# A fused four-layer kernel on one core: its first loads made anew, and two first-layer products in a row

## The chip, the cores and the metric

The kernel runs on one core of a Trainium2 chip. The metric is the device time of one execution in microseconds. The core has five engines with a queue each: TensorE (PE in the profile; its weight loads are a row of their own, PEld), VectorE (DVE), ScalarE (ACT), GpSimd (POOL) and SyncE (SP, which here only issues transfers). Transfers (DMAs) are issued from the queues of SP, ACT and POOL.

## The reference, cut to what matters

There are 64 sequences of 64 tokens, 512 wide, in float32. Four layers follow each other, each with a residual:

```python
x = x + einsum('bsi,bio->bso', x, W[id]) + b[id][:, None, :]          # layer 0: one of 16 weight matrices per sequence
x = x + x @ W1.T + ((x @ A[ad].T) @ Bm[ad].T) * scal[ad]               # layer 1: shared weight, rank-16 adapter per sequence
q, k, v = x @ Wq.T, x @ Wk.T, x @ Wv.T                                 # layer 2: attention
q, k = rope(rms(q), kv_len + t), rope(rms(k), kv_len + t)
# k, v are written into paged caches; each token attends to the last 256 positions
x = x + softmax(q @ k_all.T * SCALE + window_mask) @ v_all @ Wo.T
x = x + x @ w3[subj] + b3[subj]                                        # layer 3: one of 8 64x64 matrices per sequence
```

Four integers per sequence steer this: the layer 0 matrix, the adapter, the layer 3 matrix, and the length of its cache. A table of 257 page numbers per sequence says where its cache lies.

## The kernel before, in words

**Tiles.** The 4096 tokens are 32 tiles of 128 tokens, two sequences each. A first half (to some 545 us) does layers 0 and 1 and the projections of layer 2; a second half does attention and layer 3. The change touches only the start of the first half.

**The order is written out by hand.** Nothing is reordered: each engine runs its instructions in the order in which the program text meets them. An instruction that waits holds up all that stands behind it in its engine's queue.

**Groups.** The tiles go in groups of 1, 1, 2, 4, 4, ... (`GROUPS`): tile 0, tile 1, tiles 2 and 3, tiles 4 to 7, and so on. Groups smaller than the next one are called short here. The main loop (L709 ff. before) takes group g through layer 1 and, spread between, the next group through layer 0. For a tile `i0` of the next group and a tile `i` of this one:

- `layer0(i0)`, L244 to 255: 8 matmuls into a PSUM bank (each is two matmul instructions, so x16 in the trace), L249; ACT copies the bank to `s0`, L252; POOL adds the bias to x into `x1`, L260 (`add_bias`).
- `turn0(i0)`, L267 to 274: PE transposes `s0` (L273), DVE adds it to `x1` (L274). Only now is layer 0 of the tile done.
- `turn_x2(i)` (L654) transposes the layer 1 output; `product` (L140) multiplies it by `wq` for an earlier tile (`pq`) and by `wkv` (`pk`); `keep_kv(i)` and `parts_q` norm and rotate k and q (L120 to L135: ACT, DVE and POOL in turns).
- `layer1(tiles)`: the adapter's first product `pxa` (L620) needs `x1` of every tile of the group; DVE masks it into `xa` (L625); `p1 = x1 @ w1` (L635); the adapter's second product adds `bo @ xa` (L643); ACT copies the bank out (L648).

Where a group is short, some tiles of the next one have no `i`; there `turn0(i0)` follows `layer0(i0)` at once, and PE's transposes wait for ACT's copy of `s0`.

**Side work on DVE.** `rotation(0)` (L366 to 397) makes the sine and cosine for tiles 0 to 7, 20 DVE instructions and two on ACT; `scalars()` (L399 to 407) prepares the norm's gains. `windows()` (L427 ff.) is a generator that computes from the page tables which cache rows to fetch; `other(i)` (L697) takes two of its steps per tile: in the trace its set-up and 5 "picks" (L470) stand with tile 1, 10 picks with tile 2, 11 with tile 3.

**Loads and their order.** SP's queue issues the integers (`tok1`, L198), x of tile 0 (L222), then weights: for tile 0 in four chunks per sequence (`load_w0(0, KC, (nc.sync, nc.scalar))`), the first sequence's from SP, the second's from ACT. Then `w1`, adapter rows (`ao`, L293), x and weights of tile 1, `wkv`, and so on. ACT's queue first issues four small loads: `idcol` (the 64 matrix numbers, one per partition, L200), `toki` (all 256 integers, to all 128 partitions, L202), `invf` (L204) and `gain` (L205); after the weights come `kvi` and `tabi` (L322 and L323). POOL gathers the bias rows `brow` (L212, needs `idcol`) and the adapter rows `bo` (L301, needs `toki`).

Transfers of SP and ACT share eight completion semaphores in turn, in the order of the program text. The ninth transfer reuses the first one's, so its issue waits until that one has landed.

Of the kernel before, what the change touches and what calls it, by code (L numbers as in the profile page):

```python
# [22 lines left out]
KC = D // 128  # L23
# [36 lines left out]
def body(ctx: ExitStack, tc: tile.TileContext, a: dict, out: bass.AP):  # L60
# [124 lines left out]
    with ExitStack() as pa:  # L185
# [13 lines left out]
        idcol = su.tile([B, 1], I32, name="idcol")  # L199
        nc.scalar.dma_start(idcol, a["toks"][:, 0:B].rearrange("o b -> b o"))  # L200
        toki = su.tile([128, 4, B], I32, name="toki")
        nc.scalar.dma_start(toki.rearrange("p k b -> p (k b)"), a["toks"].partition_broadcast(128))  # L202
        invf = su.tile([128, HALF], F32, name="invf")
        nc.scalar.dma_start(invf, a["invf"].partition_broadcast(128))  # L204
        nc.scalar.dma_start(  # L205
            gain.rearrange("p k h f -> p (k h f)"), a["gains"].partition_broadcast(128)
        )
        make_identity(nc, ident)
        pidx = su.tile([128, 1], I32, name="pidx")
        P.iota(pidx, pattern=[[0, 1]], base=0, channel_multiplier=1)  # L210
        brow = su.tile([B, D], F32, name="brow", tag="valp")
# [12 lines left out]
        def load_w0(i, parts=1, queues=(nc.sync, nc.sync)):  # L224

            w0s[i] = []
            for b, queue in zip((2 * i, 2 * i + 1), queues):
                w = wp.tile([128, KC, D], F32, name="w")
                r = queue.value_load(tok1[0:1, 0, b : b + 1], min_val=0, max_val=E - 1)
                for n in range(parts):  # L230
                    cs = slice(n * KC // parts, (n + 1) * KC // parts)
                    queue.dma_start(
                        w[:, cs], a["W0"][bass.ds(r, 1)].rearrange("a (c p) o -> p (a c) o", p=128)[:, cs]
                    )
                w0s[i].append(w)
# [7 lines left out]
        def layer0(i, bias=True):  # L243

            p0 = bank("p0")
            for c in range(KC):
                for h in range(2):
                    hs = slice(h * T, (h + 1) * T)
                    TE.matmul(p0[hs, :], xs[i][:, c, hs], w0s[i][h][:, c, :], start=c == 0, stop=c == KC - 1)  # L249
            w0s.pop(i)  # L250
            s0 = s0s[i] = wk.tile([128, D], F32, name="s0")
# [15 lines left out]
        def turn0(i):  # L267
# [4 lines left out]
            for c in range(KC):  # L272
                TE.transpose(pt[:, c * 128 : (c + 1) * 128], s0[:, c * 128 : (c + 1) * 128], ident)  # L273
            V.tensor_tensor(x1, pt.rearrange("p (c t) -> p c t", c=KC), x1, ALU.add)  # L274
# [43 lines left out]
        kvi = su.tile([128, 1], I32, name="kvi")  # L318
        tabi = su.tile([128, NBLK], I32, name="tabi")
        for h in range(2):  # L320
            hs = slice(h * B, (h + 1) * B)
            nc.scalar.dma_start(kvi[hs], a["toks"][:, 3 * B :].rearrange("o b -> b o"))  # L322
            nc.scalar.dma_start(tabi[hs], a["tab"])  # L323
# [26 lines left out]
        V.tensor_copy(adf.rearrange("p o q -> p (o q)"), toki[:, 1, :])  # L350
        V.tensor_tensor(adf, adf, bc(mine[:, None, :], [128, 8, 8]), ALU.mult)
# [47 lines left out]
        def scalars():  # L399
# [210 lines left out]
        bg, old, turns, asked, made = windows(), copies(kvd[:OLD], op, 3), {}, [], []  # L610

# [54 lines left out]
        scalars()  # L666

        biasT = su.tile([128, KC, B], F32, name="biasT")
        layer0(0, False)
        pb = bank("pb")  # L670
        for c in range(KC):
            TE.transpose(pb[:, c * B : (c + 1) * B], brow[:, c * 128 : (c + 1) * 128], ident[:B, :B])
        S.copy(biasT.rearrange("p c b -> p (c b)"), pb[:, : KC * B])
        add_bias(0)
        turn0(0)
# [21 lines left out]
        def other(i):  # L697

            next(bg, None)
# [378 lines left out]
```

## Time and profile before

| what | us |
|---|---|
| median of 9 runs | 951.18 (950.16 to 953.06) |
| the profiled execution | 950.0 |
| its span, first to last instruction | 948.0 |
| PE busy | 921.0 |
| DVE busy | 613.1 |
| ACT busy | 415.2 |
| POOL busy | 404.8 |

A span is the time from the first instruction to the last; 2.0 us of the profiled execution lie around it. In the rows of the timeline a line has the start in us, the length, the engine, the line of the kernel, the operation, what it writes and reads (buffer numbers left out), the shapes, how many instructions were merged, and in brackets how long the engine was idle before and what ended that. `p` is the bank of layer 0 (L249) or of layer 1 (L635, L643); `w` is any weight tile. PEclk is the granted share of TensorE's clock.

### The profile page before, as it was taken

The numbers are of one execution on the slowest core, as the hardware profiler recorded it, in microseconds if no ns is written. First come the engines' busy times: TensorE is split into PE (matmuls) and PEld (weight loads), VectorE is DVE, ScalarE is ACT, GpSimd is POOL, SyncE is SP. The second block draws the span as 40 slices with busy tenths as digits, with TensorE's granted clock in tenths as the row PEclk, the third lists the DMA queues.
The fourth block names the chain that finished last, engine by engine and source line by source line (L and its number), as shares of the span: only waits on it lengthen the run. The fifth ranks groups of instructions, "written<-read, shape, count | busy, mean of one in ns | idle before, by whom it ended". The sixth has DMA issues, their size and how long they took to land.

```text
span 948.0 us, 17784 instructions
## 1 busy us (share of the span) xinstructions
PE 921.0 (97%) x5397; PEld 506.6 (53%) x5397; DVE 613.1 (65%) x1736; ACT 415.2 (44%) x1084; POOL 404.8 (43%) x599
## 2 busy tenths in 40 slices
PE   5999998999999999999999999999999999999998
PEld 2343443444444444444344466766666777776665
DVE  3765898888575254441324888777777777777773
ACT  0312143122243221441213386666666666666663
POOL 3343466465544353444434464444444444444400
PEclk9999999999999999999999999999999999999999
DMA  7988999999999999999982696576666666666621
GB/s 241 363 298 304 363 403 290 389 401 317 380 385 355 384 337 380 395 350 371 403 297 111 193 326 216 174 231 201 214 199 199 199 204 204 204 207 209 209 60 46
DMA packets 133344, 260.97 MB, mean 275 GB/s; under 512 B 32737, under 2 KB 41570, under 8 KB 133250
## 3 DMA queue, kind: packets, MB, share of 16 engines
q1 hardware_dynamic: 108562, 178.61, 52.5%
q0 software_dynamic: 23280, 79.84, 25.6%
q10 hardware_dynamic: 1408, 1.39, 0.5%
q8 instruction: 43, 0.70, 0.3%
q14 instruction: 51, 0.42, 0.1%
HBM read 190.29 MB, written 69.50 MB: 274 GB/s over the span
## 4 chain that ended last, share of the span: by engine, by line
PE 72%; DVE 2%; DMA 1%; ACT 0%; issue 0%; POOL 0%; ACTq 0%
PE py L917 12%; PE po L889 8%; PE ps L842 8%; PE p L635 7%; PE pq L140 7%; PE pk L140 7%; PE ppt L875 6%; PE p L249 6%; PE pkt L823 2%; PE ppt L879 1%; PE pkt L829 1%; PE pz L929 1%; DMA w<-in_W 1%; PE pqt L174 1%; PE px L654 1%; PE pt L273 1%
## 5 line engine op out<-in xcount | busy, mean ns | idle before, releaser
L769 POOL DMA_INDIRECT kv<-kvd,idxn x128 | 126.6, 989 | 189.6 <-PE po L889 128.4
L854 ACT ACTIVATE pr<-pr,mx 128x320 f32<-128x320 f32 x256 | 140.1, 549 | 21.0 <-DVE mx L850 21.0
L249 PE MATMUL p<-w,xt 128*64 128x512 f32 x512 | 122.6, 605 | 9.3 <-DMA w<-in_W 9.3
L850 DVE CUSTOM_DVE_ANT_0 pr<-ps,mb 128x320 f32<-128x320 f32 x256 | 107.8, 487 | 25.7 <-PE ps L842 25.6
L917 PE MATMUL py<-wo,oT 128*128 128x512 f32 (+1 forms) x264 | 118.3, 591 | 1.7 <-DVE qn L128 1.7
L140 PE MATMUL pk<-wkv,x 128*128 128x512 f32 x256 | 115.4, 595 | 2.1 <-ACT x L656 2.1
L155 POOL DMA_INDIRECT st<-in_kvc,cidx x68 | 69.8, 1027 | 106.8 <-DMA kvd<-st 97.7
L635 PE MATMUL p<-w,x 128*128 128x512 f32 x256 | 113.2, 599 | 0.0
L140 PE MATMUL pq<-wq,x 128*128 128x512 f32 x248 | 111.3, 593 | 0.0
L274 DVE TENSOR_TENSOR x<-pt,x 128x512 f32<-128x512 f32 x32 | 22.0, 688 | 101.6 <-PE pt L273 91.6
L866 DVE TENSOR_SCALAR pr<-pr,sm 128x320 f32<-128x320 f32 x256 | 85.3, 395 | 2.2
L889 PE MATMUL po<-pT,kv 128*64 128x128 f32 (+1 forms) x1536 | 82.1, 278 | 0.0
L917 PEld LDWEIGHTS py<-wo,oT 128*128 128x128 f32 x264 | 47.5, 189 | 61.5 <-issue 58.4
L842 PE MATMUL ps<-kT,qT 64*128 64x320 f32 x512 | 79.2, 443 | 1.2 <-issue 1.2
L635 PEld LDWEIGHTS p<-w,x 128*128 128x128 f32 x256 | 48.2, 191 | 58.7 <-issue 56.8
L889 PEld LDWEIGHTS po<-pT,kv 128*64 128x64 f32 (+1 forms) x1536 | 68.9, 135 | 19.8 <-DVE mx L850 13.6
L249 PEld LDWEIGHTS p<-w,xt 128*64 128x64 f32 x512 | 35.5, 137 | 80.0 <-issue 72.7
L135 POOL TENSOR_TENSOR qr<-qn,sq 128x512 f32<-128x512 f32 x25 | 31.7, 1268 | 106.8 <-DVE qn L134 106.8
L140 PEld LDWEIGHTS pk<-wkv,x 128*128 128x128 f32 x256 | 46.3, 190 | 50.4 <-issue 47.3
L140 PEld LDWEIGHTS pq<-wq,x 128*128 128x128 f32 x248 | 44.9, 190 | 46.2 <-issue 46.2
L123 ACT ACTIVATE ss<-ss,epst 128x4 f32<-128x4 f32 (+1 forms) x64 | 19.1, 299 | 110.5 <-DVE ss L122 110.4
L133 DVE TENSOR_TENSOR sq<-qn,sg 128x256 f32<-128x256 f32 (+1 forms) x128 | 40.1, 355 | 40.2 <-POOL sg L110 37.5
(191 smaller groups left out, 1352.9 us busy)
## 6 DMA issues: line engine op xcount, KB each, us to landing
w<-in_W SPq DMA_DIRECT2D x62, 1024.0 KB
kvd<-st SPq DMA_DIRECT2D x68, 512.0 KB
xt<-in_xT SPq DMA_DIRECT2D x32, 256.0 KB
x2d<-x2n SPq DMA_DIRECT2D x32, 256.0 KB
kvd<-kvn SPq DMA_DIRECT2D x32, 256.0 KB
qTd<-qTs SPq DMA_DIRECT2D x32, 256.0 KB
qT<-qTd SPq DMA_DIRECT2D x32, 256.0 KB
x2r<-x2d SPq DMA_DIRECT2D x32, 256.0 KB
```

The lines of the kernel that those rows point to most:

```text
L140: TE.matmul(ps, x2s[i][:, c, :], w[:, c, :], start=c == 0, stop=c == KC - 1)
L155: P.indirect_dma_start(out=st, out_offset=None, in_=a["kvc"].rearrange("(n r) d -> n (r d)", r=2), in_offset=bass.IndirectOffsetOnAxis(ap= ...
L249: TE.matmul(p0[hs, :], xs[i][:, c, hs], w0s[i][h][:, c, :], start=c == 0, stop=c == KC - 1)
L635: TE.matmul(p1[i], x1s[i][:, c, :], w1[:, c, :], start=c == 0, stop=False)
L769: P.indirect_dma_start(out=kv[:, n, :], out_offset=None, in_=kvd, in_offset=bass.IndirectOffsetOnAxis(ap=at, axis=0),)
L842: TE.matmul(ps[g2][:, :NPOS], qT[rows, gp, b2].rearrange("p h t -> p (h t)"), kT[rows, gp, b2 * NPOS : (b2 + 1) * NPOS], start=True, stop= ...
L850: V.tensor_tensor_reduce(out=p, in0=ps[g2][:, :NPOS], in1=mb[:, b2, :], scale=-1.0, scalar=3.0e38, op0=ALU.add, op1=ALU.min, accum_out=mx[ ...
L854: S.activation(p, p, AF.Exp, bias=mx[:, g, b2 : b2 + 1], scale=-1.0, accum_out=sm[:, g, b2 : b2 + 1],)
L866: V.tensor_scalar(p, p, sm[:, g, b2 : b2 + 1], None, ALU.mult)
L875: TE.transpose(pt[:, n * 128 : (n + 1) * 128], pr[:, g, at : at + 128], ident)
L889: TE.matmul(po[b2][g2 * 64 : (g2 + 1) * 64, gp * 128 : (gp + 1) * 128], kv[rows, n, (G + g) * HD : (G + g + 1) * HD], pT[rows, c, m * 128 ...
L917: TE.matmul(py[:, fs], oT[:, c].rearrange("p b t -> p (b t)"), wo[:, c, fs], start=c == 0, stop=c == KC - 1,)
```

## The change

All line numbers here are of the kernel before.

- **The integers are spread by TensorE.** `idcol`, `toki` and `kvi` are loaded no more. DVE copies `tok1` to float32, four matmuls against a row of ones spread it over the partitions of a PSUM bank (`ptok`), and DVE copies two columns out or reads the bank itself.
- **Small loads last.** `invf`, `gain` and `tabi` move from ACT's queue to SP's, behind `wkv`. ACT's queue issues only its four chunks of the first weights.
- **First weights by chunk in turns.** `load_w0` with parts issues chunk 0 of both sequences, then chunk 1, and so on. On each queue the order stays as it was; the order in which the eight semaphores are given out changes.
- **Bias rows turned earlier.** The transposes of `brow` go ahead of the last chunk's matmuls of tile 0 (`turn_bias`); `turn0(0, 2)` transposes and adds in two halves.
- **Side work moved.** `scalars()` but for three operations, and `rotation(0)`, go from between `layer1([0])` and `layer0(1)` to behind `turn0(1)`. `windows()` takes no step with tile 1 and four with tile 2.
- **Two layer 0 runs in a row.** Where there is no `i`, the tile's `turn0` is held back until the next tile's `layer0` and `turn_x2` are out: for tiles 2, 4 and 6. `s0` gets two buffers.

```diff
         nc.sync.dma_start(tok1.rearrange("p k b -> p (k b)"), a["toks"])
-        idcol = su.tile([B, 1], I32, name="idcol")
-        nc.scalar.dma_start(idcol, a["toks"][:, 0:B].rearrange("o b -> b o"))
-        toki = su.tile([128, 4, B], I32, name="toki")
-        nc.scalar.dma_start(toki.rearrange("p k b -> p (k b)"), a["toks"].partition_broadcast(128))
-        invf = su.tile([128, HALF], F32, name="invf")
-        nc.scalar.dma_start(invf, a["invf"].partition_broadcast(128))
-        nc.scalar.dma_start(
-            gain.rearrange("p k h f -> p (k h f)"), a["gains"].partition_broadcast(128)
-        )
         make_identity(nc, ident)
...
+        one = su.tile([1, 128], F32, name="one")
+        V.memset(one, 1.0)
+        tokf = su.tile([1, 4, B], F32, name="tokf")
+        V.tensor_copy(tokf, tok1)
+        ptok = bank("ptok")
+        TE.matmul(ptok[:B, 4 * B : 4 * B + 1], tokf[:, 0, :], one[:, :1], start=True, stop=True)
+        for h in range(2):
+            TE.matmul(
+                ptok[h * B : (h + 1) * B, 4 * B + 1 : 4 * B + 2], tokf[:, 3, :], one[:, :1], start=True, stop=True
+            )
+        TE.matmul(ptok[:, : 4 * B], one, tokf.rearrange("p k b -> p (k b)"), start=True, stop=True)
+        toki = ptok[:, : 4 * B].rearrange("p (k b) -> p k b", k=4)
+        idcol = su.tile([B, 1], I32, name="idcol")
+        V.tensor_copy(idcol, ptok[:B, 4 * B : 4 * B + 1])
+        kvi = su.tile([128, 1], I32, name="kvi")
+        V.tensor_copy(kvi, ptok[:, 4 * B + 1 : 4 * B + 2])
...
+            first = [row(h) for h in range(2)] if parts > 1 else []
+            for n in range(parts):
+                cs = slice(n * KC // parts, (n + 1) * KC // parts)
+                for h in range(2):
+                    r = first[h] if first else row(h)
+                    queues[h].dma_start(
+                        w0s[i][h][:, cs],
+                        a["W0"][bass.ds(r, 1)].rearrange("a (c p) o -> p (a c) o", p=128)[:, cs],
                     )
...
             for c in range(KC):
+                if c == KC - 1 and not bias:
+                    turn_bias()
                 for h in range(2):
...
-        def turn0(i):
+        def turn0(i, parts=1):
...
+            for n in range(parts):
+                lo, hi = n * KC // parts, (n + 1) * KC // parts
+                for c in range(lo, hi):
+                    TE.transpose(pt[:, c * 128 : (c + 1) * 128], s0[:, c * 128 : (c + 1) * 128], ident)
+                V.tensor_tensor(
+                    x1[:, lo:hi], pt[:, lo * 128 : hi * 128].rearrange("p (c t) -> p c t", t=128), x1[:, lo:hi], ALU.add
+                )
...
         load_weight(wkv, "wkvT")
-        kvi = su.tile([128, 1], I32, name="kvi")
+        invf = su.tile([128, HALF], F32, name="invf")
+        nc.sync.dma_start(invf, a["invf"].partition_broadcast(128))
+        nc.sync.dma_start(gain.rearrange("p k h f -> p (k h f)"), a["gains"].partition_broadcast(128))
         tabi = su.tile([128, NBLK], I32, name="tabi")
         for h in range(2):
-            hs = slice(h * B, (h + 1) * B)
-            nc.scalar.dma_start(kvi[hs], a["toks"][:, 3 * B :].rearrange("o b -> b o"))
-            nc.scalar.dma_start(tabi[hs], a["tab"])
+            nc.sync.dma_start(tabi[h * B : (h + 1) * B], a["tab"])
...
-            V.memset(epst, EPS)
-            V.tensor_tensor(eye2, ident[:, :64], ident[:, 64:], ALU.add)
-            scale_b(0)
-
+
+        V.memset(epst, EPS)
+        V.tensor_tensor(eye2, ident[:, :64], ident[:, 64:], ALU.add)
+        scale_b(0)
...
-        scalars()
...
         layer0(0, False)
...
         add_bias(0)
-        turn0(0)
+        turn0(0, 2)
...
         def other(i):
 
-            next(bg, None)
-            next(bg, None)
+            for _ in range(0 if i == 1 else 4 if i == 2 else 2):
+                next(bg, None)
...
             layer1(tiles[g])
-            if g == 0:
-                run(rotation(0))
-            elif g == 1:
+            if g == 1:
                 far()
...
-                if i is not None:
-                    turn_x2(i)
-                q = asked.pop() if asked and i is not None else None
+                if i is None:
+
+                    held.append(i0)
+                    continue
+                turn_x2(i)
+                if held:
+                    turn0(held.pop())
+                q = asked.pop() if asked else None
                 if q is not None:
                     pq = product(q, wq, "pq")
                 turn0(i0)
+                if g == 0:
+                    scalars()
+                    run(rotation(0))
...
```

More of the change, by code (lines that the diff above doesn't have):

```diff
@@ L224, in load_w0, with row @@
         def load_w0(i, parts=1, queues=(nc.sync, nc.sync)):
[L226 to L233, printed above, removed]
+            w0s[i] = [wp.tile([128, KC, D], F32, name="w") for _ in range(2)]
+            def row(h):
+                b = 2 * i + h
+                return queues[h].value_load(tok1[0:1, 0, b : b + 1], min_val=0, max_val=E - 1)
+            first = [row(h) for h in range(2)] if parts > 1 else []
[6 more added lines that the diff above has]
+                        a["W0"][bass.ds(r, 1)].rearrange("a (c p) o -> p (a c) o", p=128)[:, cs],
                     )
-                w0s[i].append(w)
         def load_next(i):
@@ L250, in layer0 @@
             w0s.pop(i)
-            s0 = s0s[i] = wk.tile([128, D], F32, name="s0")
+            s0 = s0s[i] = wk.tile([128, D], F32, name="s0", bufs=2)
             S.copy(s0, p0)
@@ L271, in turn0 @@
             pt = bank("pt")
-            for c in range(KC):
-                TE.transpose(pt[:, c * 128 : (c + 1) * 128], s0[:, c * 128 : (c + 1) * 128], ident)
-            V.tensor_tensor(x1, pt.rearrange("p (c t) -> p c t", c=KC), x1, ALU.add)
+            for n in range(parts):
[5 more added lines that the diff above has]
+                )
         w1 = wts.tile([128, KC, D], F32, name="w1")
@@ L349, in body @@
         adf = su.tile([128, 8, 8], F32, name="adf")
-        V.tensor_copy(adf.rearrange("p o q -> p (o q)"), toki[:, 1, :])
-        V.tensor_tensor(adf, adf, bc(mine[:, None, :], [128, 8, 8]), ALU.mult)
+        V.tensor_tensor(
+            adf, toki[:, 1, :].rearrange("p (o q) -> p o q", q=8), bc(mine[:, None, :], [128, 8, 8]), ALU.mult
+        )
         ado = su.tile([128, 8], F32, name="ado")
@@ L610, in body @@
         bg, old, turns, asked, made = windows(), copies(kvd[:OLD], op, 3), {}, [], []
+        held = []
         def layer1(tiles):
@@ L663, in keep_kv, with turn_bias @@
             nc.sync.dma_start(kvd[OLD + i * 128 : OLD + (i + 1) * 128], kvn)
-        scalars()
         biasT = su.tile([128, KC, B], F32, name="biasT")
+        def turn_bias():
+            pb = bank("pb")
+            for c in range(KC):
+                TE.transpose(pb[:, c * B : (c + 1) * B], brow[:, c * 128 : (c + 1) * 128], ident[:B, :B])
+            S.copy(biasT.rearrange("p c b -> p (c b)"), pb[:, : KC * B])
         layer0(0, False)
[L670 to L673, printed above, removed]
         add_bias(0)
-        turn0(0)
+        turn0(0, 2)
         load_next(0)
@@ L732, in body @@
                     made.append(q)
-                if i is not None:
-                    keep_kv(i, product(i, wkv, "pk"), P)
-                    if i < NT - LATE:
-                        asked.append(i)
-                    if len(made) > 1:
-                        turn_q(made.pop(0))
+                keep_kv(i, product(i, wkv, "pk"), P)
+                if i < NT - LATE:
+                    asked.append(i)
+                if len(made) > 1:
+                    turn_q(made.pop(0))
         layer1(tiles[-1])
```

## The prediction

> **What bounds the kernel now.** I read the page first, then TensorE's rows in the timeline for idle times, then the stages of the start, then VectorE's rows.
>
> ```profile
> PE 921.0 (97%) x5397; PEld 506.6 (53%) x5397; DVE 613.1 (65%) x1736; ACT 415.2 (44%) x1084; POOL 404.8 (43%) x599
> ...
> PE 72%; DVE 2%; DMA 1%; ACT 0%; issue 0%; POOL 0%; ACTq 0%
> ```
>
> The page: PE is busy 97% of the span and carries 72% of the chain that ended last. So a change gains by PE's idle time or not at all. PE's rows of the first 106 us (an idle time stands in the bracket):
>
> ```profile
> 8.35 5.77 PE L249 MATMUL p<-w,xt 128*64 128x512 f32 x12 [8.35 <-DMA w<-in_W]
> 14.70 1.43 PE L249 MATMUL p<-w,xt 128*64 128x512 f32 x4 [0.58 <-DMA w<-in_W]
> ...
> 19.36 1.92 PE L620 MATMUL pxa<-x,ao 128*32 128x128 f32 x8 [1.90 <-DVE x L274]
> 21.21 4.41 PE L635 MATMUL p<-w,x 128*128 128x512 f32 x8
> 25.55 1.12 PE L643 MATMUL p<-bo,xa 32*128 32x512 f32 x2
> 26.61 4.68 PE L249 MATMUL p<-w,xt 128*64 128x512 f32 x16
> ...
> 40.83 1.12 PE L643 MATMUL p<-bo,xa 32*128 32x512 f32 x2
> ...
> 46.30 0.66 PE L273 MATMUL pt<-ident,s 128*128 128x128 f32 x4 [0.77 <-ACT s L252]
> ...
> 58.45 1.10 PE L620 MATMUL pxa<-x,ao 128*32 128x128 f32 x16
> ...
> 72.02 0.66 PE L273 MATMUL pt<-ident,s 128*128 128x128 f32 x4 [0.77 <-ACT s L252]
> ...
> 89.89 0.66 PE L273 MATMUL pt<-ident,s 128*128 128x128 f32 x4 [0.77 <-ACT s L252]
> ...
> 103.85 1.09 PE L620 MATMUL pxa<-x,ao 128*32 128x128 f32 x26 [1.02 <-DVE x L274]
> ```
>
> Idle PE here: 8.35 us until the first weights, 0.58 between them, 1.90 until DVE has finished tile 0's layer 0, three times 0.77 for ACT's copy of `s0` in the short groups, and 1.02 before tiles 4 to 7's `pxa`, for DVE. The rest of the run has some 9 us, which the change does not touch.
>
> The stages of the start (columns: stretch, its length, busy us of each engine with instructions, granted clock, DMA share, GB/s):
>
> ```profile
> 2.00:5.00 3.00, 0.00 (x0) 0.00 (x0) 0.00 (x0) 0.00 (x0) 1.22 (x2) 1.00 0.44 135
> 5.00:9.00 4.00, 0.65 (x1) 0.29 (x2) 3.09 (x16) 0.00 (x0) 1.00 (x2) 1.00 0.79 259
> ...
> 18.00:20.00 2.00, 0.64 (x3) 0.54 (x4) 1.39 (x4) 0.00 (x0) 1.46 (x5) 0.82 0.32 83
> 19.30:22.70 3.40, 3.34 (x10) 2.07 (x11) 2.85 (x10) 0.00 (x0) 2.40 (x5) 0.50 0.93 276
> 20.00:45.00 25.00, 24.85 (x83) 9.92 (x80) 18.12 (x69) 6.74 (x11) 6.92 (x13) 0.95 1.04 376
> ```
>
> From 2 to 5 us the transfers run at 135 GB/s, at 259 until 9, at 83 from 18 to 20, against 376 later. In the trace's semaphore updates tile 0's eight chunks land from 8.2 to 15.0. SP's waits show why: it holds chunks back for `toki` (1.3 us) and `invf` (1.4 us), whose semaphores they reuse, and tile 1's weights for `w1` (2.1 us). One row has PE at half clock, from 19.3 to 22.7. There `pxa` took 1.92 us (tile 1's, at full clock, 1.09) and `p1` 4.41 (3.70): 1.5 us lost.
>
> VectorE's rows:
>
> ```profile
> 18.61 0.69 DVE L274 TENSOR_TENSOR x<-pt,x 128x512 f32<-128x512 f32 x1 [3.06 <-POOL x L260]
> ...
> 21.53 0.40 DVE L375 TENSOR_TENSOR ang<-pos,invf 128x256 f32<-128x256 f32 x1
> ...
> 28.80 0.29 DVE L395 TENSOR_SCALAR cos<-cos 128x256 f32<-128x256 f32 x1
> ...
> 34.01 0.69 DVE L274 TENSOR_TENSOR x<-pt,x 128x512 f32<-128x512 f32 x1
> ...
> 40.11 0.28 DVE L625 TENSOR_TENSOR xa<-pxa,own 32x128 f32<-32x128 f32 x1
> ...
> 55.31 0.69 DVE L274 TENSOR_TENSOR x<-pt,x 128x512 f32<-128x512 f32 x1
> ```
>
> The reader should see that from 21.5 to 29.1 DVE makes tile 0's rotation **while PE is busy** with `p1` and tile 1's layer 0, and then, until 34.0, the window set-up and 5 picks. This work costs no PE time now. Tile 3's `x1` is done at 56.0, 2.4 us before `pxa` at 58.45 wants it.
>
> **The change part by part.**
>
> *First loads.* Without the small loads, the chunks issue at 3.1 to 4.8 us (0.56 apart, as SP's first two), and none waits for a small load. x of tile 0 took 2.8 us from issue to landing, so the first chunk lands at about 5.6, the rest each 0.68 us later (0.26 MB at 385 GB/s, between the 376 above and the 392 of 11 to 15 us), the last near 10.7 with the bias rows. The four spreading matmuls and two casts are not in the trace: between 0.5 us (the four transposes of `brow`, 0.46) and 1.5 (the `pst` matmul 1.0, two DVE copies). I take 1.2: `tok1` lands at 2.1, `idcol` is there at 3.5, the gather issues at 3.6 against 3.65, lands at some 10 to 11 (10.98 now), and the turned bias holds the last chunk by 0.5 us at most. Layer 0 of tile 0 then ends at 12.0 (16.1). `bo` is issued at 6.2 instead of 8.0 and takes 7.05 us as now: 13.2, plus its scaling 0.5. Copy, transposes and two half adds end no earlier than 14.0; behind the scaling, 14.5, against 19.3.
>
> *To the end of tile 1's layer 0.* `w1` lands at 13.9, `ao` at 14.6. `pxa` 1.1, `p1` 3.7, `bo` 1.1 bring PE to tile 1 at 20.5. Its weights: 5.97 MB since 4.4 us at 376 to 392 GB/s, plus 0.3 to land, 19.9 to 20.6. Layer 0 takes 3.65, end **24.3**, against 31.3: 7.0 us earlier. Bounds: 23.5 (transfers at 400 GB/s, `bo` 0.8 earlier) and 25.8 (another half-clock stretch, 1.5).
>
> *Rotation, gains and windows moved.* DVE now stands idle while PE does all that, and starts after tile 1's add, which ends 2.15 us after layer 0 (31.3 to 33.4, had the picks not held it): 26.4. Then, in queue order: four gain operations 1.0; rotation 7.56 (21.53 to 29.09); ACT's cosine 0.45; square, reduce, table load and root, norm and `xa` 4.10 (36.29 to 40.39). `xa` of tile 1 ends at 39.5. But PE finishes tile 1's `p1` at 24.3 + 9.6 = 33.9 and waits at the adapter matmul **5.6 us**; now that matmul runs at 40.83 without a wait. Behind the gains' load on DVE stand rotation, `keep_kv` and `xa`; it lands near 25, 1.4 us before its turn. ACT's copy of tile 1 stands behind the sine, and is not due before.
>
> Next is the tile 2 and 3 stretch. From `xa` to the end of tile 3's add DVE takes 15.61 us now (40.39 to 56.00, with a 1.82 wait for POOL's `um`, which stays). The set-up and 5 picks come on top, 5.09 us (29.00 to 34.09). Tile 3's `x1` is done at 39.55 + 15.61 + 5.09 = **60.3**. Unhindered PE would reach this `pxa` 16.9 us after the adapter matmul, at 56.4. It starts at 60.3 against 58.45: **+1.9**. All 7 us are spent and more: from the end of layer 0 of tile 1, DVE's queue needs 2.15 + 33.8 us, PE's own work 26.4.
>
> *Runs of two.* Each takes 0.77 us of PE. The first is worth nothing, as PE waits for DVE anyway. The second (tiles 4, 5) counts: +1.1. In the third DVE's rows are solid from tile 5's add (81.77) to tile 7's (103.80), the order only exchanges within, and PE waits there already; the 0.77 lengthens that wait from 1.0 to 1.8. Net stays **+1.1**. After that PE has the same work as before.
>
> *SP's queue.* Four small issues (0.5 us each) now stand before x and weights of tile 2, which wait for the semaphore of tile 1's weights. Weights of tile 2 land near 31, wanted at 40; of tile 3 near 42 (13.65 MB), wanted at 44. Cost nothing; if the transfers ran 2 us later, the wait of 60.3 would still cover it.
>
> *The clock.* Before the half-clock row, PE was busy 1.3 of 3.4 us, with 1.9 and 0.3 idle. The new idle times are 5.6 (40 us), 2 to 4 (60 us) and 1.8 us (105 us). Half clock after the first is hidden by the wait at 60. After the second it is not: between 0 and the measured 1.5 us; the wait is longer than the one that had it, so I take 1.5. The third, shorter than 1.9, I take as none, up to 1.5.
>
> The sum: 1.1 + 1.5 = **+2.6**. The profiled execution would go from 950.0 to 952.6; the median of 951.18 lies 1.18 above that execution, so 953.8.
>
> [...]
>
> **The rivals.**
>
> 1. *DVE sets the time, but no half clock is paid*, or the loads come at the bound of 23.5. Then +1.1, or +0.3: 951.5 to 952.3. For it: 1.55 us of idle PE at 154 us brought no half clock. Against it: the row at 19.3.
> 2. *Faster: DVE's run is shorter.* From 26.4 to tile 3's add I need 33.8 us; below 30.8 the whole gains more than 0.2%. One thing could do it: the engines' waits within the run, 1.82 for `um` and 1.28 for ACT's table load, gone together. Without any DVE limit the gain would be 7.0 + 3 x 0.77 + 1.0 = 10.3 us, 940.9; half of the way, 946. Against it: POOL's iotas stand behind `kvn` and the table alternates between sine and root, in the old order as in the new.
> 3. *The loads come no earlier*: the gathers wait for the spread integers and hold the last chunk, so layer 0 of tile 1 ends at 27 or later. Then the DVE run starts 2.7 us later: +3.8, with half clock +5.3, 955 to 956.5. Against it: `idcol` takes about as long as its load now, 3.4 us.
>
> **How the numbers follow.** A measurement of this kernel can tell about 0.2%, 1.9 us, from no change. The forecast (DVE's queue with a half-clock stretch, or two) has 0.56, rival 1 has 0.28, rival 2 has 0.09, rival 3 has 0.07. Slower by over 0.2%: forecast and rival 3, 0.63, of which I move 0.02 to no change, as the forecast's lower end is just at the bound: 0.61. Within 0.2%: 0.30. Faster: 0.09. The likeliest is 953.8; its own range is 952.3 to 955.5. The range downwards takes in rival 1 with loads at their bound and a DVE run shorter by 1.2 us (the picks of 44 to 47 us, 0.54 each with POOL busy beside them, at the others' 0.47: 0.5; and 0.7 of the `um` wait), 950.3; upwards rival 3 with half clock, 956.5.
>
> **What would show it.** Right: first weights landed by 11 us and tile 1's layer 0 over near 24; DVE idle some 9 us before tile 1's add and then without pause to 60; the adapter matmul (L664 after) idle 5 to 6 us for `xa`; tiles 2 and 3's `pxa` (L641) idle 2 to 4 us for DVE; no 0.77 us before the transposes of tiles 2, 4 and 6. Wrong: no idle time at these two places, or tile 1's layer 0 still ending after 27.

## The result and the profile after

| | before | after |
|---|---|---|
| time, median (range) | 951.47 us (949.61 to 954.52, 31 runs) | 955.5 us (954.65 to 957.42, 10 runs) |
| ratio to before, 95% interval | | 1.0043 [1.0034, 1.0052] |
| profiled execution, span | 948.0 us | 952.5 us |
| PE busy | 921.0 us | 925.1 us |
| start of the adapter matmul of tile 0 / tile 1 / tiles 2 and 3 | 25.55 / 40.83 / 66.54 | 20.58 / 40.15 / 68.69 |
| of tiles 4 to 7 / tiles 8 to 11 / tiles 12 to 15 | 118.80 / 185.38 / 251.37 | 119.96 / 190.88 / 256.07 |
| first score matmul of the second stage | 544.92 | 549.44 |

The changed kernel is 0.43% slower; 953.8 us was forecast. The page after, PE's busy line and the shares of the chain that ended last:

```profile
PE 925.1 (97%) x5405; PEld 508.5 (53%) x5405; DVE 613.5 (64%) x1740; ACT 415.4 (44%) x1084; POOL 402.8 (42%) x599
...
PE 71%; DVE 2%; DMA 1%; ACT 0%; issue 0%; SPq 0%; POOL 0%; ACTq 0%
```

PE still carries the chain, with 4 us more of busy time: 1.73 us of it are the new spreading matmuls, and more of the old work than before ran at half clock: the granted clock was 0.50 for 10.24 us, before for 3.41. PE's rows after (start, length, what, and in brackets the idle time before it and what ended that):

```profile
6.89 5.32 PE L264 MATMUL p<-w,xt 128*64 128x512 f32 x12 [2.69 <-DMA w<-in_W]
...
12.52 1.08 PE L264 MATMUL p<-w,xt 128*64 128x512 f32 x4
...
21.63 3.65 PE L264 MATMUL p<-w,xt 128*64 128x512 f32 x16
...
40.15 2.07 PE L664 MATMUL p<-bo,xa 32*128 32x512 f32 x2 [5.25 <-DVE xa L646]
42.15 9.00 PE L264 MATMUL p<-w,xt 128*64 128x512 f32 x32
...
60.01 0.44 PE L641 MATMUL pxa<-x,ao 128*32 128x128 f32 x2 [0.53 <-DVE x L291]
...
69.75 7.09 PE L264 MATMUL p<-w,xt 128*64 128x512 f32 x32
...
91.91 3.65 PE L264 MATMUL p<-w,xt 128*64 128x512 f32 x14 [0.92 <-DMA w<-in_W]
...
141.62 0.66 PE L290 MATMUL pt<-ident,s 128*128 128x128 f32 x4 [0.99 <-ACT s L267]
...
156.03 0.66 PE L290 MATMUL pt<-ident,s 128*128 128x128 f32 x4 [2.17 <-ACT s L267]
158.23 5.40 PE L140 MATMUL pk<-wkv,x 128*128 128x512 f32 x8 [1.54 <-ACT x L677]
```

The reader should see three things. PE starts on the first weights 1.5 us earlier (6.89 against 8.35), and tile 1's layer 0 ends at 25.28 instead of 31.3. All but 0.7 us of that is spent in one wait of 5.25 us at tile 1's adapter matmul. And a new loss stands far behind the change, at 141 to 164 us, where before PE had waited 0.84 and 1.54 us and run at full clock (1.00 from 152.0 to 158.2 us):

```profile
152.23 0.66 PE L273 MATMUL pt<-ident,s 128*128 128x128 f32 x4 [0.84 <-ACT s L252]
154.43 3.70 PE L140 MATMUL pk<-wkv,x 128*128 128x512 f32 x8 [1.54 <-ACT x L656]
```

A profile is one execution, and the start of this kernel is not the same in each: two later profiles (the runs with held and with thinned copies) have the same program up to some 65 us, and tile 0's adapter matmul starts at 22.82 and 21.75 us in them, against 20.58 here.

The clock, from the stages after (columns: stretch, its length, busy us of each engine with instructions, granted clock, DMA share, GB/s):

```profile
35.80:39.20 3.40, 0.00 (x0) 0.00 (x0) 1.40 (x5) 2.52 (x5) 0.58 (x2) 1.00 1.05 382
39.20:46.00 6.80, 5.85 (x12) 1.74 (x14) 4.61 (x25) 0.58 (x1) 5.93 (x12) 0.50 0.41 132
155.27:158.68 3.41, 1.11 (x5) 0.71 (x6) 3.31 (x6) 3.37 (x6) 2.52 (x4) 1.00 0.88 294
158.70:162.10 3.40, 3.40 (x5) 1.33 (x4) 3.37 (x4) 1.27 (x1) 2.94 (x4) 0.50 0.72 241
```

PE runs at half clock from 39.2 to 46.0 us, after a stretch with no matmul at all, and again from 158.7 to 162.1, after a stretch in which it was busy 1.11 of 3.41 us. In the first the two matmuls took 2.07 instead of 1.12 us and tiles 2 and 3's layer 0 9.00 instead of the 7.09 that tiles 4 and 5's takes; in the second eight matmuls took 5.40 instead of 3.70.

VectorE's rows after, from its long idle time to the tiles of the next group:

```profile
26.76 0.69 DVE L291 TENSOR_TENSOR x<-pt,x 128x512 f32<-128x512 f32 x1 [8.85 <-PE pt L290]
...
39.81 0.28 DVE L646 TENSOR_TENSOR xa<-pxa,own 32x128 f32<-32x128 f32 x1
41.91 0.46 DVE L713 TENSOR_SCALAR um<-um 128x576 f32<-128x576 f32 x1 [1.82 <-POOL um L711]
...
59.27 1.29 DVE L291 TENSOR_TENSOR x<-pt,x 128x512 f32<-128x512 f32 x2
...
111.50 0.76 DVE L133 TENSOR_TENSOR sq<-qn,sg 128x256 f32<-128x256 f32 x2 [4.65 <-POOL sg L110]
```

and POOL's row that VectorE waits for at the end of it:

```profile
109.89 0.95 POOL L155 DMA_INDIRECT st<-in_kvc,cidx  x1 [11.13 <-DMA kvd<-st]
110.86 0.34 POOL L110 TENSOR_TENSOR cg<-gain,cos 128x64 f32<-128x64 f32 x1
111.13 0.33 POOL L110 TENSOR_TENSOR sg<-gsw,sin 128x64 f32<-128x64 f32 x1
```

The same places before:

```profile
106.23 0.96 POOL L155 DMA_INDIRECT st<-in_kvc,cidx  x1 [8.38 <-DMA kvd<-st]
```

```profile
107.84 0.76 DVE L133 TENSOR_TENSOR sq<-qn,sg 128x256 f32<-128x256 f32 x2 [2.15 <-POOL sg L110]
```

POOL's sixth gather of the old cache needs one of five buffers (`st`), and the first comes free when the first store of the old cache has landed. The gain products for the next norm (`cg`, `sg`, L110) stand behind it on POOL's queue, and VectorE's norm waits for them. That wait has grown from 2.15 to 4.65 us. The experiments below ask what it is worth.

### The profile page after: what moved, and what is told of

Same layout as the page of the kernel before. It is cut to its first block, busy times and chain, and to the rows that moved or that the text cites. A ratio compares the mean times of both kernels' runs of the same rounds, so it can differ in the third digit from the quotient of the medians.

```text
span 952.5 us, 17801 instructions
## 1 busy us (share of the span) xinstructions
PE 925.1 (97%) x5405; PEld 508.5 (53%) x5405; DVE 613.5 (64%) x1740; ACT 415.4 (44%) x1084; POOL 402.8 (42%) x599
## 4 chain that ended last, share of the span: by engine, by line
PE 71%; DVE 2%; DMA 1%; ACT 0%; issue 0%; SPq 0%; POOL 0%; ACTq 0%
PE py L945 12%; PE po L917 8%; PE ps L870 8%; PE p L656 7%; PE pq L140 7%; PE pk L140 7%; PE ppt L903 6%; PE p L264 6%; PE pkt L851 2%; PE ppt L907 1%; PE pkt L857 1%; PE pz L957 1%; DMA w<-in_W 1%; PE pqt L174 1%; PE px L675 1%; PE pt L290 1%
## 5 line engine op out<-in xcount | busy, mean ns | idle before, releaser
L291 DVE TENSOR_TENSOR x<-pt,x 128x512 f32<-128x512 f32 (+1 forms) x33 | 22.0, 672 | 103.1 <-PE pt L290 96.1
```

## The experiments

Three readings were open. **Theory D**: VectorE's own work (rotation, lists, norms) sets the time, in the stretch to 105 us as forecast and again behind it. **Theory T**, later **theory C**: behind 105 us it is the copies of the old cache, by transfers and by POOL's queue. And the question of which part of the change gives and which takes.

### The parts: rotation back, moves alone, runs of two alone, loads alone

Rotation and scalars back at their old place, with all else of the change (`invf` and gains then load on ACT's queue behind its four chunks, `tabi` ahead of `wkv`):

```diff
+        invf = su.tile([128, HALF], F32, name="invf")
+        nc.scalar.dma_start(invf, a["invf"].partition_broadcast(128))
+        nc.scalar.dma_start(gain.rearrange("p k h f -> p (k h f)"), a["gains"].partition_broadcast(128))
...
-            for _ in range(0 if i == 1 else 4 if i == 2 else 2):
+            for _ in range(1 if i == 1 else 3 if i == 2 else 2):
...
+            if g == 0:
+                scalars()
+                run(rotation(0))
-                if g == 0:
-                    scalars()
-                    run(rotation(0))
```

> The changed kernel, but tile 0's rotation and the gains go back to their old place behind layer 1 of tile 0; for that their two loads are issued from ACT's queue right behind its weight chunks, the page table's load goes ahead of wkv, and the window work takes 1, 3, 2, 2 steps at tiles 1 to 4 instead of 0, 4, 2, 2. Theory D (VectorE's queue eats the early start): no idle TensorE at tile 1's adapter matmul nor at tiles 2 and 3's adapter product for VectorE; some of the 6 to 7 us won at tile 1's layer 0 stays, up to where the weights of tile 3 land (42.8 us in the changed kernel): about 3.5 to 5 us faster than before, 946.5 to 948. Rival L (the new loads and their order cost) and rival P (the runs of two cost): the kernel stays near the changed one, 953 to 956.

Measured: 949.71 us (12 runs), ratio 0.9986 [0.9972, 1.0001], span 946.4. That is far from the rivals' 953 to 956, but theory D's 946.5 to 948 was missed as well.

The kernel before with only these moves:

```diff
-        scalars()
...
-            next(bg, None)
-            next(bg, None)
+            for _ in range(0 if i == 1 else 4 if i == 2 else 2):
+                next(bg, None)
...
-            if g == 0:
-                run(rotation(0))
-            elif g == 1:
+            if g == 1:
...
+                if g == 0:
+                    scalars()
+                    run(rotation(0))
```

> The kernel before, in which only the rotation, the gains and the window steps move as in the change; loads and runs as before. Theory D: tile 1's add ends at 33.4 us, VectorE needs 33.8 more to tile 3's add, 67.2, so tiles 2 and 3's adapter product starts 8.8 us later than now, and the end is 9 to 12 us later: 960 to 963. Rivals L and P: within 1 us of before, 950.5 to 952.5.

Measured: 960.06 us (6 runs), ratio 1.0100 [1.0081, 1.0118], span 957.8. PE's rows at tile 1's adapter matmul, at tile 2's layer 0 and at tiles 2 and 3's `pxa`:

```profile
46.52 2.07 PE L643 MATMUL p<-bo,xa 32*128 32x512 f32 x2 [5.52 <-DVE xa L625]
48.52 6.56 PE L249 MATMUL p<-w,xt 128*64 128x512 f32 x16
...
67.91 1.10 PE L620 MATMUL pxa<-x,ao 128*32 128x128 f32 x16
```

The time is the expected one, the path is so only in part. The granted clock was 0.50 for 10.24 us, from 44.17 us on, so the adapter matmuls and tile 2's layer 0 took 3.9 us longer (2.07 and 6.56 us instead of 1.12 and 3.65). With that, PE reached tiles 2 and 3's `pxa` 1.1 us after VectorE's last add, which ended at 66.79, and did not wait there.

The kernel before with only the runs of two (two buffers for `s0`, and the held `turn0`):

```diff
-                if i is not None:
-                    turn_x2(i)
-                q = asked.pop() if asked and i is not None else None
+                if i is None:
+                    held.append(i0)
+                    continue
+                turn_x2(i)
+                if held:
+                    turn0(held.pop())
+                q = asked.pop() if asked else None
```

> The kernel before with the runs of two alone. Theory D: two of the three idle times of 0.77 us are won, the third goes into a longer wait for VectorE at 103 us: 1.5 us faster, 949.5 to 950.5. Rival P (two layer 0 in a row ask for weights earlier than they land, or hold transfers back): slower, 952.5 to 955.

Measured: 951.87 us (12 runs), ratio 1.0012 [1.0000, 1.0025], span 947.4. The gain of 1.5 us did not come, nor did rival P's loss.

The kernel of the first experiment without the runs of two, so the loads alone:

```diff
-                if i is None:
-                    held.append(i0)
-                    continue
-                turn_x2(i)
-                if held:
-                    turn0(held.pop())
-                q = asked.pop() if asked else None
+                if i is not None:
+                    turn_x2(i)
+                q = asked.pop() if asked and i is not None else None
```

> The new first loads alone, without the runs of two, rotation and scalars at the old place, copies as in the kernel before. If the lead of the first call's 949.71 us came from the loads and the runs gave nothing, 949.5 to 950.3, ahead by 3 us at the adapter matmul of tiles 4 to 7 and by less than 1 us at that of tiles 8 to 11. If the runs of two carried it, 951 to 951.5.

Measured: 950.07 us (12 runs), ratio 0.9989 [0.9972, 1.0005], span 949.7. The time lies in the range given for the loads, the leads do not: 1.85 us instead of 3 at the first of the two places, and 2.50 behind at the second.

Lead (minus) or lag against the profile of before at the adapter matmuls, us:

| | tile 1 | tiles 4 to 7 | tiles 8 to 11 | first scores |
|---|---|---|---|---|
| moves alone | +5.69 | +9.47 | +11.04 | +9.90 |
| runs of two alone | +0.58 | -1.25 | -0.30 | -0.56 |
| loads alone | -2.19 | -1.85 | +2.50 | +1.66 |
| loads and runs, rotation back | -3.68 | -4.03 | -0.42 | -1.65 |
| the whole change | -0.68 | +1.16 | +5.50 | +4.51 |

Each row is one execution, and so is the profile of before. The runs of two can't act before 42 us, and their +0.58 at tile 1 is scatter: that execution had 6.83 us of half clock at the start where before had 3.41. Differences of about 1 us in this table are therefore not told from scatter.

What follows. The moves are what makes the change slower: alone they cost 9.5 us by 119 us, 5.5 of it the wait and 3.9 the half clock behind it, and on top of loads and runs 5.2 (-4.03 to +1.16). VectorE stands idle where it had made the rotation beside PE's work, and makes it later, while PE waits. Without the moves the changed kernel would be 0.6% faster by the two ratios (0.9986 against 1.0043), but no more than even with the kernel before. For whatever has been won by 119 us is lost again by 185: loads and runs lose 3.6 of their 4.0 us there, the runs alone 1.0 of 1.25, the loads 4.4. The expectation for the runs (949.5 to 950.5) missed for this reason, and the changed kernel loses another 4.3 us in the same group.

### The gathers of tile 4, one step later

The kernel before, none of the old cache's gathers at tile 4 and three at tile 5:

```diff
-                for _ in range(2 - i % 2):
+                for _ in range({4: 0, 5: 3}.get(i, 2 - i % 2)):
                     next(old, None)
```

> The kernel before, in which the first two cache gathers are given out one tile later (none at tile 4, three at tile 5), so some 3 us later, out of the time in which few transfers run. Theory T (the 3.3 us that the changed kernel loses between 105 and 165 us come through the transfers, as its gathers start 4.6 us later into a stage where transfers run full): 1 to 3.5 us slower, 952.5 to 955, with the later gathers and the norm behind them late. Rival (this loss comes from TensorE and VectorE being late themselves): no change, 951 to 952.

Measured: 951.46 us (12 runs), ratio 1.0003 [0.9991, 1.0016]. This is the rival's 951 to 952, but inconclusive as a test of the transfers, since the edit moved the first gathers by 1.7 us only, against 4.6 in the changed kernel. It left one useful pair: VectorE's wait for `sg` 2.64 us (2.15 before), the group 66.87 us (66.58).

### The copies held back

The next three hold all copies of the old cache back until tile 12, and then give 3.5 gathers for each tile instead of 2.5; nothing is left out.

```diff
                 if i > 3:
 
                     next(bg, None)
+                if i > 11:
                     next(old, None)
...
-            if i > 3:
-                for _ in range(2 - i % 2):
+            if i > 11:
+                for _ in range(3 - i % 2):
                     next(old, None)
```

> The changed kernel with the copies of the old cache held back: no gather before tile 12, then three and a half for each tile instead of two and a half (nothing is left out, the same 68 gathers and stores). So POOL's queue has no gather that waits for a store before about 185 us, and some 7 MB less is moved before 160 us. It is to be read beside the kernel before with the same edit (next run). Theory C (the lateness that the first gathers inherit from VectorE, passed on through POOL's queue and the transfers, adds the 3.3 us that the change loses between 105 and 165 us): 1.0 to 1.5 us behind its partner at the adapter matmul of tiles 4 to 7 and no more than 2 us behind it at that of tiles 8 to 11 and in the time; PE's waits for s0 copies at 141 and 156 us under 0.5 us each. Theory D (VectorE's own work, the lists and norms, is late by itself, copies or not): still 4 to 5 us behind its partner at the adapter matmul of tiles 8 to 11 and in the time.

> The kernel before with the same hold on the copies, the partner of the run above. Theory C: PE's wait for ScalarE's copy at 152 us (0.84 us) and the loss after 120 us go, 949 to 951 if nothing is lost later; where the denser copies after 185 us collide with the weights' loads, 951 to 954. Theory D: 951, no change.

> The changed kernel with rotation and scalars at the old place (949.71 us in the first call, 4.0 us ahead of the kernel before at the adapter matmul of tiles 4 to 7, and only 0.4 us ahead at that of tiles 8 to 11), and the copies held as above. Theory C: the 4 us stay: 3 to 4 us ahead of the kernel before with held copies at both places and in the time, 946 to 948. Theory D: the lead is again lost by the adapter matmul of tiles 8 to 11, 0.5 to 1.5 us ahead in the time, 949.5 to 950.5.

Measured: 1058.71, 1061.47 and 1054.48 us, ratios 1.114, 1.116 and 1.110. In the times all three expectations failed by 100 us, as no reading had asked what 3.5 gathers for each tile do. Yet the stretch that was in question answers. From the adapter matmul of tiles 4 to 7 to that of tiles 8 to 11 the three took 64.14, 64.12 and 64.14 us, where the same kernels with their copies take 70.92, 66.58 and 70.18. Against the kernel before with held copies, the changed one stood 2.94 us behind at the first of the two places (1.0 to 1.5 was expected; its start was late in this execution) and 2.96 at the second; the one with the rotation put back 4.78 ahead and 4.77. Neither gain nor lag changes in this group any more: theory C, and against theory D, since VectorE's lists were all there.

After 185 us the same mechanism shows at full size. The rows of POOL, VectorE and PE of the kernel before with held copies, at 237 to 243 us:

```profile
236.70 0.94 POOL L155 DMA_INDIRECT st<-in_kvc,cidx  x1 [14.32 <-DMA kvd<-st]
```

```profile
238.29 0.76 DVE L133 TENSOR_TENSOR sq<-qn,sg 128x256 f32<-128x256 f32 x2 [15.19 <-POOL sg L110]
```

```profile
242.67 1.12 PE L273 MATMUL pt<-ident,s 128*128 128x128 f32 x4 [14.81 <-ACT s L252]
```

One gather waits 14.32 us for a store to land; the gains behind it hold VectorE for 15.19, ScalarE's copy comes late by that, and PE stands for 14.81 us. It has such a wait of 14.8 to 16.0 us in every group up to 521 us, and from 265 us on a second one of 7.6 to 9.1. The first such group takes 81 us for its four tiles and the next three 92 to 93, instead of 64.

### The copies thinned at one place

To take the wait away without the pile-up, none of the gathers is issued with the first product of tiles 4 to 7 and none with tile 7. Five have then been issued before tile 8, as many as there are buffers.

```diff
                 if i > 3:
 
                     next(bg, None)
+                if i > 7:
                     next(old, None)
...
-                for _ in range(2 - i % 2):
+                for _ in range(0 if i == 7 else 2 - i % 2):
                     next(old, None)
```

> The changed kernel with rotation and scalars at the old place (949.71 us in the first call), and the old-cache gathers thinned at one place only: none with the adapters' first product of tiles 4 to 7 and none with tile 7, so that five have been issued before tile 8 (as many as there are buffers) and none waits for a store on POOL's queue before 125 us; from tile 8 on one for each first product and two or one for each tile, as in the kernel before (69 places for 68 gathers). Theory C (the gathers that wait for stores on POOL's queue at 105 to 128 us delay the norms, and those PE at 140 to 165 us): the group from the adapter matmul of tiles 4 to 7 to that of tiles 8 to 11 takes 64 to 65 us (70.18 without the edit), the lead of 4 us stays, and the time is 945 to 947. Theory D (VectorE's lists and norms are late without the copies too): 949 to 950. Should the later copies be the next limit, the lead is given back after 185 us, to be seen at the later groups.

> The changed kernel with the same thinning. Theory C: the group from 120 to 191 us takes 64 to 65 us (70.92 without the edit); 1.2 to 3 us behind the kernel before with the same thinning at the adapter matmul of tiles 8 to 11 and in the time, 950 to 952. Theory D: 955, no change.

> The kernel before with the same thinning, the partner of the two above. Theory C: the group from 119 to 185 us takes 64 to 65 us (66.58 without the edit), 948.5 to 950 in the time. Theory D: 951.

Measured: 980.37, 987.47 and 981.96 us, ratios 1.0055 [1.0037, 1.0072], 1.0119 [1.0088, 1.0150] and 1.0079 [1.0056, 1.0101]. These ran on another chip, on which the kernel before took 974.38 us, so the ratios are to be read and not the times. The group took 64.24, 64.26 and 64.21 us, as theory C had it. PE's rows of the changed kernel with this edit have none of the three waits at 141 to 158 us left but a rest of the last, while the weights of tile 7 still come late (first row):

```profile
93.59 3.65 PE L264 MATMUL p<-w,xt 128*64 128x512 f32 x14 [1.46 <-DMA w<-in_W]
...
154.41 3.70 PE L140 MATMUL pk<-wkv,x 128*128 128x512 f32 x8 [0.28 <-ACT x L678]
```

At the first scores the three stood 5.70 ahead, 4.79 behind and 3.21 ahead of the profile of before (the changed one had lost 4 us more at 413 us, to a wait and to half clock; its mean granted clock is 0.981, that of the two others 0.991). But the lead does not reach the end, and in the times all three expectations failed. In the kernel before with this edit the last three gathers now lie at 511 to 519 us (the last of before at 489), and POOL's first load of the cache for the second stage starts at 530.39 us, against 525.85, although PE is 3.2 us ahead. Right behind its first four score matmuls PE stands:

```profile
550.44 3.57 PE L843 MATMUL ps<-kT,qT 64*128 64x320 f32 x12 [7.91 <-issue]
```

The changed kernel with this edit has a wait of 9.16 us at the same matmuls, and half clock stands behind the first scores: the granted clock from 540 to 600 us, in three stretches of 20 us, was 0.74, 0.96 and 0.87 in the kernel before with this edit and 0.83, 0.74 and 1.00 in the one with the rotation put back, some 17 us of half clock in each, where the profile of before has 1.00 throughout. By the ratio the kernel before with this edit ends 0.8%, 7.7 us, late. How much of it is the late load and how much this chip was not separated: no profile of the kernel before was taken there.

### The thinned copies given back early

With the rotation at its old place, the five gathers given back as a second one with each odd tile from 9 to 17:

```diff
-                for _ in range(0 if i == 7 else 2 - i % 2):
+                for _ in range(0 if i == 7 else 2 if 8 < i < 18 else 2 - i % 2):
                     next(old, None)
```

> The changed kernel with rotation and scalars at the old place and the same thinning before tile 8, but the five gathers given back early: two instead of one with each odd tile from 9 to 17 (74 places for 68 gathers, as in the kernel before), so that the last copies lie where they lay and the load of the cache for the second stage isn't late. If the loss of the thinned kernels after 540 us came from their last copies lying at 511 to 519 us, it is gone here and the lead at 540 us (5.7 us) reaches the end: ratio 0.993 to 0.996 to the kernel before on the same chip. If the loss has another cause, or the added gathers make POOL wait as the held copies did after 185 us: ratio 1.000 to 1.006, in the second case with PE's waits for ScalarE's copies between 185 and 320 us.

Measured: 957.79 us (6 runs), beside 951.07 for the kernel before on the same chip, ratio 1.0063 [1.0046, 1.0080]. The second case of the expectation came true, at the upper end of its range. The lead is 5.37 us at the adapter matmul of tiles 8 to 11, and the next group takes 73.54 us instead of some 65:

```profile
217.53 0.66 PE L290 MATMUL pt<-ident,s 128*128 128x128 f32 x4 [2.99 <-ACT s L267]
...
232.74 0.66 PE L290 MATMUL pt<-ident,s 128*128 128x128 f32 x4 [1.29 <-ACT s L267]
```

Later groups lose 1 to 2 us each, and the second stage starts 8.40 us late and loses nothing more (8.39 at its last quarter). So the second stage did not suffer here, where the last copies lie early; that speaks for the late load as the cause above, though this is another chip. And two and a half gathers for each tile seem to be about what the first stage carries: in this run five more, spread over nine tiles, cost more than the wait that they were to save. No version was found that beats the kernel before clear of the noise.

### What the wait is worth

All profiles in one table: the wait of POOL's gather for the first store, VectorE's wait for `sg` behind it, and the length of the group that follows (adapter matmul of tiles 4 to 7 to that of tiles 8 to 11), in us:

| kernel | POOL | VectorE | half clock in the group | group |
|---|---|---|---|---|
| copies held, thinned or given back, seven kernels | none | none | none | 64.12 to 64.30 |
| before | 8.38 | 2.15 | none | 66.58 |
| gathers of tile 4 later | 8.88 | 2.64 | none | 66.87 |
| runs of two alone | 9.56 | 3.09 | none | 67.52 |
| moves alone | 8.56 | 2.33 | 3.41 | 68.14 |
| loads and runs, rotation back | 10.83 | 4.36 | 3.41 | 70.18 |
| loads alone | 10.54 | 4.31 | 6.83 | 70.92 |
| the whole change | 11.13 | 4.65 | 3.41 | 70.92 |

64.2 us and VectorE's wait give 66.35, 66.84 and 67.29 for the three rows without half clock, within 0.25 of what was measured; the rows with half clock are 1.6 to 2.4 us above their sum. The wait counts in full because VectorE has no idle time left behind it: up to 163 us the changed kernel's VectorE has no wait of over 0.6 us. Each window step of this group (`hit` and `own`, L555 and L559) takes 2.5 us, and the norms and adds that PE needs stand among them in queue order; in the changed kernel ScalarE waits 5.16 us for VectorE's sum of squares at 135.87 us, before 2.66 us, and its copies of `s0`, in order behind that, reach PE late. The difference is 2.50 us, as much as VectorE's wait for `sg` has grown. After and then before:

```profile
135.87 0.30 ACT L123 ACTIVATE ss<-ss,epst 128x8 f32<-128x8 f32 x1 [5.16 <-DVE ss L122]
```

```profile
132.20 0.30 ACT L123 ACTIVATE ss<-ss,epst 128x8 f32<-128x8 f32 x1 [2.66 <-DVE ss L122]
```

Two things lengthen the wait. Where PE and VectorE come earlier (loads, runs), the store does not come earlier with them: in "loads and runs" VectorE reaches the place 4.3 us earlier (101.39 against 105.69 us) and the gather that waits for the store issues 2.1 us earlier (104.15 against 106.23). In the changed kernel VectorE comes 1.16 us later (106.85) and the gather 3.66 us later. There the first gathers stand behind the picks, which run until tile 3's add: the gathers go out at 69.81, 71.11 and 73.69 us (before 65.25, 66.54 and 69.12), and the first stores are issued at 96.58 us instead of 94.01. Meanwhile the transfers stood still for 5 us, as their rate in 40 slices of 1 us from 60 to 100 us shows, after and then before:

```profile
GB/s 389 389 166 0 0 0 0 0 102 176 16 70 190 410 350 365 399 348 410 393 390 389 399 395 379 389 385 393 387 387 331 150 23 314 277 270 188 252 289 289
```

```profile
GB/s 365 404 410 397 387 389 391 402 422 336 375 393 389 385 342 277 377 365 410 403 401 385 389 385 389 387 345 190 25 33 123 367 274 135 129 399 418 416 381 401
```

The load that wasn't moved at 63 to 72 us is then moved at 73 to 90, in front of the stores. That this is why the store takes 13.3 us instead of 12.2 to free its buffer is argued from these rows and was not tried by itself.

## Why the prediction was right, and where not

The forecast was slower, by 2.6 us; it is slower by 4.0 (4.5 in the profiled executions). The sign and the cause up to 105 us stand. Against the profile the sum misses 1.9 us: its +1.1 came out in this pair of profiles and not in two others, its +1.5 was put in the wrong place, and the largest loss stands where it had no term.

- **First loads: right in kind, short in size.** The last chunk was to land near 10.7 and landed, by the semaphore updates, at 11.83, layer 0 of tile 0 was to end at 12.0 and ended at 13.60, tile 1's at 24.3 and ended at 25.28, inside the bounds of 23.5 and 25.8. The spreading matmuls were mis-sized: the term for them was 1.2 us, but the one for all integers alone took 1.22, so `idcol` was there at 4.2 us and not 3.5, and all behind it moved. This execution is the best of the three with the same start: in the profiles with held and with thinned copies tile 1's layer 0 ended at 27.5 and 26.4, outside the bounds, 3.6 and 4.6 us earlier than in their partners where 7.0 was forecast. The 0.3 us "to land" in the sum for tile 1's weights was the author's estimate; no run shows it by itself, and PE began on these weights at 21.63 without a wait. PE's rows with held copies show a wait for the bias rows, tile 0's layer 1 at half clock (5.14 us instead of 3.70), and the late layer 0 of tile 1:

```profile
12.52 0.43 PE L694 MATMUL pb<-ident,brow 64*128 64x64 f32 x4 [0.26 <-DMA brow<-in_b,idcol]
...
17.75 5.14 PE L656 MATMUL p<-w,x 128*128 128x512 f32 x8
...
23.87 3.65 PE L264 MATMUL p<-w,xt 128*64 128x512 f32 x16
```

- **VectorE's solid run: right.** Tile 1's add was to end at 26.4 and the run to take 33.8 us to 60.3. It ended at 27.4 and took 33.1, to 60.5. That tile 1's adapter matmul would wait 5.6 us: 5.25. The experiments with the moves alone (+9.47) and the moves taken back (-5.2) confirm that these moves, and no load, are its cause. Rival 2, a shorter run, is out. Rival 3 is out in this profile, but not in kind: with held copies the bias rows did hold the last chunk, and layer 0 of tile 1 ended at the 27 or later that it names.
- **Net +1.1 at 105 us: measured +1.16,** but that it agrees to 0.1 us is luck. Against their partners the changed kernels with held and with thinned copies stand 2.94 and 2.47 us behind at the same place, where no copy had yet made anything wait. And +1.16 is made up otherwise than the third pair's term. The two pairs' 0.77 came off. The third was said to be eaten by a wait of 1.8 us for VectorE before tiles 4 to 7's `pxa`. That wait was 0.16 (1.02 before), as PE came late: 0.92 us for weights of tile 7 stand at 91.91 us. With the copies held back the weights are in time, and the wait is there with 1.71. The step on SP's queue, "cost nothing", holds for the weights of tiles 2 and 3 that it spoke of; those of tile 7, which it did not look at, came late after the stretch without transfers.
- **Half clock, +1.5 after the wait at 60 us: wrong.** The wait there was put at 2 to 4 us and was 0.53 and 0.16. That a wait of such a length is followed by half clock was the author's estimate, from the one row at 19.3. The half clock after the first wait was to be hidden by this one, and it was, but it then lasted two stretches (6.83 us) and used the second wait up. In the changed kernel with thinned copies it lasted 10.24 us (tiles 2 and 3's layer 0 took 9.87 us, against 7.09 for that of tiles 4 and 5), and no wait was left at tiles 2 and 3's `pxa` to hide it in. The half clock that did cost time stands behind the waits of 2.17 and 1.54 us before 158.23: PE was busy for 1.11 of the 3.41 us from 155.27, and the granted clock was 0.50 from 158.7 to 162.1.
- **"After that PE has the same work as before": this is the step that failed.** The work is the same and its start is not. In the group behind 120 us PE loses 4.34 us against before: 2.5 by VectorE's longer wait for POOL's gains and 1.7 by the half clock at 158.7; 0.1 is not accounted for. Later groups give 0.8 to 1.0 back. That the end came close to the forecast is partly luck: the +1.1 came out in one pair of three, the +1.5 was not paid where it had been put, and 3.3 us came in that no step had named.

## What to carry to other kernels

A gain at the start counts only as far as the next place where another queue sets the pace: here an in-order POOL queue, whose ring of five buffers waits for stores to land, took back 3.6 of 4.0 us. Before costing a move at "the same work as before", follow each queue to its next wait for a buffer, and look whether the engine behind that wait has idle time left; if not, the wait counts in full, as it did here to within 0.25 us in three kernels. And an edit that thins such a queue at one place must say where the work goes: here half a gather more for each tile, over nine tiles, cost 7 to 8 us, and one more for each tile, from tile 12 on, cost over 100.

## What the runs showed of the hardware

- The granted clock was 0.50 for 3.41 us behind a stretch in which PE was busy for 1.11 of 3.41 us (after, from 155.27 us), for 1.31 of 3.41 (before, from 15.86) and for 1.38 of 3.41 (rotation back, from 149.63). That cost 1.5 us in the kernel before (`pxa` 1.92 us instead of 1.09, `p1` 4.41 instead of 3.70) and 1.7 in the two others (eight matmuls 5.40 us instead of 3.70). It was 0.50 for 6.8 us behind a stretch without a matmul (after, from 35.80 to 39.20). Behind stretches with 1.86 (before, from 152.38) and 2.00 us (after, from 151.85) of 3.41 the next 3.41 us had 1.00. No bound in busy time comes out of these few.
- The same instructions had a different clock in different executions. Up to 42 us the kernel before, the same with runs of two and the same with thinned copies (on another chip) run the same program; they had 3.41, 6.83 and 0 us of half clock there.
- A store of 512 KB of the old cache took 12 to 13 us from its issue to the release of its buffer (before: 94.01 to 106.2, after: 96.58 to 109.9), with two loads of 1 MB issued just ahead of it.
- The same kernel took 974.38 us on one chip and 950.6 to 951.5 on the others. Two profiles from there have PE waiting 2.5 us (the kernel before with thinned copies) and 3.1 us (rotation back with thinned copies) between 740 and 840 us for a copy of `pT` that causes no wait in the profiles of before and of the loads alone (0.0 us before the same matmuls). Why was not looked into.
